# A gated MLP of a perceiver block: part of gate and up by seven products of halves, and a triangular substitution in two halves of rows

## The chip, the cores and the metric

One core of one Trainium2 chip runs the whole program in one launch. The time is the device time of one execution in microseconds (us); before the change three runs gave 2789.46 to 2791.44 us, median 2791.18. A core has a matmul engine (TensorE, in the profile PE, with its weight loads listed apart as PEld), VectorE (DVE), ScalarE (ACT), GpSimd (POOL), and SyncE (SP), which here only issues DMAs. Each engine takes its instructions in order. On-chip memory is SBUF (128 partitions) and PSUM, eight banks of 512 fp32 values per partition, where matmuls write.

## What is computed

The reference is a block of three layers over x of 128 x 32 x 512 fp32 values (4096 tokens of 512 channels), each added to x:

```python
x = x + _L0_xattn_ref(_layernorm(x), mask, ctx_2048, ctx_2048, ...)   # cross-attention
x = x + _L0_attn_ref(_layernorm(x), ...)[0]                           # delta rule, then gated MLP
x = x + _L0_ffn_ref(_layernorm(x), ...)                               # quantised FFN after a Hadamard rotation
...
h2 = _rms(x, mlp_norm_w)          # the gated MLP inside the second layer
gate = h2 @ Wgate.T               # 512 -> 1408
up = h2 @ Wup.T
x = x + silu(gate) * up @ Wdown.T
```

The delta rule is a scan over 32 time steps per sequence and head. The kernel replaces the scan by a triangular system per sequence and head (32 rows, 16 values each), solved by forward substitution.

## The kernel before

All of it is fp32 apart from the quantised FFN. The program has four stages in time: cross-attention (0 to about 617 us), the products of the delta rule (`delta_products`, to about 1090), the delta rule's outputs with the gated MLP (`delta_out_mlp`, to about 2230), and the FFN (`HadamardFfn.run`, to the end). A scheduler places the instructions that the code traces into each engine's queue, mostly in traced order, but earlier where an engine would idle. `InOrder` ties the calls that go through it to the traced order; `follow` ties two instructions; `tc.issue_after` puts what is traced in its block behind a given instruction on that instruction's engine. `mixed` interleaves generators: each yields the cost of the step that it just traced, and the one that is furthest behind its own total goes next.

The MLP stage goes over 16 blocks of 256 tokens (`TB`), two tiles of 128 each. `mlp(b)` holds the work of a block: for each of 11 chunks of 128 hidden channels (`FC`) four matmuls of gate into one PSUM tile (L1307), four of up into another (L1310), SiLU on ACT (L1312) and the product into `mT` on VectorE (L1313); then for each of the two tiles 11 matmuls of down (L1318), the addition of the input (L1323), statistics, the subtraction of the mean (L1328), two butterfly steps of the Hadamard transform (`butterflies`, L128 and L129), and two stores on GpSimd's queue (L1325, L1330). A step's cost is 3.5 for a chunk and 9.5 for a down tile.

`back(b + 1)` prepares the next block meanwhile: it loads the solved rows `u`, copies them on GpSimd into one of two block-diagonal operands `um` (L1225), multiplies with `pe` (L1243), normalises, multiplies with `wo` (L1272), adds a layer norm of x1 whose scaling is L1267, and transposes the result into `hT` (L99, L1296), of which there are two buffers. In blocks 1 to 8 `late_products` adds the last products of the delta rule (L782 to L794).

Also mixed in, behind the last VectorE instruction of the MLP (`mark`), are the substitution steps of `Substitution.solve`: for each row s a scaling of 64 values (L745), a multiply into `pr` (L749) and a subtraction from all later rows of `W` (L755), (31 - s) x 64 values each. There are eight such solves; the first and part of the second run in the product stage (where a helper records everything as L153), the others beside the MLP at a pace of 46 cost units per block (60 in the first). `L` has one buffer of 32 rows, loaded in four pieces, `W` two. In the last three blocks the FFN weights are made ternary instead: gate and up stay in SBUF (`resident`), down goes to DRAM (`fq`) and is loaded at the start of the FFN stage (L1671).

The weights of the MLP are loaded by SyncE: `wg` (two DMAs at 1060.75 us), then `wu` (at 1102.83) and `wd`; wg is scaled by the norm weights on ACT, wu on VectorE (L1368).

`Halves` already serves cross-attention: a product of matrices as seven products of halves (Strassen's method in Winograd's form), with four sums of the weight quarters computed once (`weights`, L260 to L263) and sums of the input quarters per use (`sums`). `operands` names the pair for each product; `BANK` names the PSUM bank that it is accumulated in; after products 1, 5 and 6 ACT copies the bank.

## Time and profile before

| | us |
|---|---|
| median of three runs | 2791.18 |
| profiled execution, its own time | 2793.26 |
| its span, first to last instruction | 2791.2 |
| TensorE busy | 2741.2 (98%) |
| VectorE busy | 2110.2 (76%) |
| ACT busy | 1109.5 (40%) |
| GpSimd busy | 740.2 (27%) |
| MLP stage, one block | 71.1, without late products 69.75 |
| FFN stage, one tile of 128 tokens | 17.0 |

The profile lists, per group of instructions, the line of code, engine, operation, output and inputs with their shapes, the count, busy time and the mean duration of one, and the idle time of the engine just before them with what ended it. Matmuls overlap each other, so the mean duration of one is longer than the distance from one start to the next; the order of time shows the latter. A busy TensorE says that it had work, not that it ran at its peak. The granted clock was 0.994 in the mean. Each fp32 matmul of the code shows as two records.

### The profile page before, as it was taken

The page shows a single profiled execution, that of the slowest core. Times are in us where ns is not written, and L with a number is a line of the kernel's source. Part 1 is how long each engine was busy: PE and PEld are TensorE (multiplying, and loading weights), DVE is VectorE, ACT ScalarE, POOL GpSimd, SP SyncE. Part 2 cuts the span into 40 slices and gives each one's busy share as a digit, 9 for nine tenths or more (in the row PEclk, how much of TensorE's full clock was granted, in tenths as well). Part 3 has the DMA queues.
Part 4 walks back from the last instruction along what each step waited for, and adds up shares of the span by engine and source line. Part 5 has one row for each costly group of instructions (what it writes and reads, how often), then busy time and mean ns, then how long its engine had stood idle before and what let it go on. Part 6 is the DMA issues. An engine that isn't in the chain of part 4 may idle for free.

```text
span 2791.2 us, 49070 instructions
## 1 busy us (share of the span) xinstructions
PE 2741.2 (98%) x18590; PEld 1847.2 (66%) x18590; DVE 2110.2 (76%) x3745; ACT 1109.5 (40%) x1972; POOL 740.2 (27%) x1076
## 2 busy tenths in 40 slices
PE   7999999999999999999999999999999989999999
PEld 6777788764444444766677777777777756666665
DVE  5565655546799797887878787878445599999998
ACT  2222222227777675222222222212222156666665
POOL 3222222215888785121111222111100100000000
PEclk9999999999999999999999999999999999999999
DMA  9898987774655668414141414131223434334443
GB/s 321 300 312 292 309 300 274 272 236 107 185 160 158 179 174 267 141 57 130 61 133 59 137 59 148 45 110 46 83 87 91 139 84 84 85 84 86 90 87 71
DMA packets 347482, 421.65 MB, mean 151 GB/s; under 512 B 151408, under 2 KB 256240, under 8 KB 345072
## 3 DMA queue, kind: packets, MB, share of 16 engines
q1 hardware_dynamic: 308064, 320.69, 38.2%
q0 software_dynamic: 39184, 97.83, 11.4%
q8 instruction: 148, 2.42, 0.4%
q14 instruction: 86, 0.70, 0.1%
HBM read 284.69 MB, written 90.18 MB: 134 GB/s over the span
## 4 chain that ended last, share of the span: by engine, by line
PE 90%; DVE 6%; DMA 2%; issue 1%; ACT 0%; SPq 0%; DVEq 0%; ACTq 0%
PE ps L153 39%; PE pm L1307 11%; PE pm L1310 11%; PE pm L1318 10%; PE pp L153 10%; PE ps L1272 4%; PE ps L1243 2%; PE pg L153 2%; DVE acc L153 1%; DVE W L153 1%; DMA raw<-in_f_w_gateT_dram 1%; PE pn L153 1%; PE ps L99 1%; DVE pr L153 1%; DVE m L153 0%
## 5 line engine op out<-in xcount | busy, mean ns | idle before, releaser
L1307 PE MATMUL pm<-hT,wg 128*128 128x256 f32 x1408 | 343.3, 386 | 0.2 <-ACT hT L1296 0.2
L1310 PE MATMUL pm<-hT,wu 128*128 128x256 f32 x1408 | 334.1, 380 | 4.4 <-DVE wu L1368 3.2
L1318 PE MATMUL pm<-wd,mT 128*128 128x512 f32 x704 | 307.4, 592 | 0.0
L1307 PEld LDWEIGHTS pm<-hT,wg 128*128 128x128 f32 x1408 | 263.9, 191 | 52.5 <-issue 13.0
L1310 PEld LDWEIGHTS pm<-hT,wu 128*128 128x128 f32 x1408 | 267.1, 190 | 42.7 <-DVE wu L1368 4.2
L755 DVE TENSOR_TENSOR W<-W,pr 128x1280 f32<-128x1280 f32 (+30 forms) x206 | 250.2, 1214 | 2.6
L749 DVE TENSOR_TENSOR pr<-L,W 128x1216 f32<-128x1216 f32 (+30 forms) x205 | 244.7, 1194 | 9.1 <-DMA L<-ld 5.0
L1318 PEld LDWEIGHTS pm<-wd,mT 128*128 128x128 f32 x704 | 132.4, 190 | 153.8 <-issue 152.8
L153 PE MATMUL ps<-wq,qT 128*128 128x512 bf16 x960 | 218.7, 381 | 3.9 <-ACT t L153 3.9
L1312 ACT ACTIVATE sg<-pm 128x256 f32<-128x256 f32 x176 | 66.9, 382 | 295.7 <-PE pm L1307 271.7
L153 PEld LDWEIGHTS <-qT 128*128 128x128 bf16 x960 | 94.3, 98 | 105.9 <-issue 7.0
L1663 POOL DMA_DIRECT2D xo<-x x29 | 24.6, 849 | 506.0 <-ACT xo L153 471.5
L1313 DVE TENSOR_TENSOR mT<-pm,sg 128x256 f32<-128x256 f32 x176 | 73.8, 419 | 107.4 <-PE pm L1310 90.0
L153 DVE TENSOR_TENSOR mb<-m 128x1024 f32<-128x1024 f32 x128 | 153.3, 1218 | 0.1
L479 POOL DMA_DIRECT2D vx<-vn x256 | 126.5, 500 | 96.2 <-DVE vn L418 52.0
L153 DVE TENSOR_TENSOR m<-mb 128x1024 f32<-128x1024 f32 x128 | 150.8, 1219 | 1.2
L153 ACT ACTIVATE t<-ps,magic,qs 128x512 f32<-128x512 f32 x158 | 115.7, 781 | 46.7 <-DVE qs L153 42.3
L1286 POOL TENSOR_TENSOR xs<-xs,y 128x512 f32<-128x512 f32 x32 | 41.9, 1310 | 321.7 <-DVE y L1283 309.5
L153 PEld LDWEIGHTS ps<-hd,mT 128*128 128x128 f32 x1024 | 119.1, 192 | 6.3 <-ACT mT L153 2.1
L793 POOL TENSOR_TENSOR kk<-kk,cm 128x256 f32<-128x256 f32 x128 | 121.1, 946 | 2.8
L153 PE MATMUL ps<-hd,mT 128*128 128x128 f32 x1024 | 119.6, 275 | 1.9 <-ACT mT L153 1.9
L789 POOL DMA_DIRECT2D ld<-kk x128 | 93.6, 731 | 89.9 <-ACT kk L153 61.6
(288 smaller groups left out, 5353.3 us busy)
## 6 DMA issues: line engine op xcount, KB each, us to landing
kall<-in_ctxT_dram SPq DMA_DIRECT2D x32, 2056.0 KB
cx<-in_ctx_dram SPq DMA_DIRECT2D x32, 2048.0 KB
x<-xo POOLq DMA_DIRECT2D x64, 256.0 KB, 4.9
ld<-kk POOLq DMA_DIRECT2D x128, 128.0 KB, 2.7
pd<-kk POOLq DMA_DIRECT2D x128, 128.0 KB, 2.6
L<-ld SPq DMA_DIRECT2D x32, 512.0 KB
pe<-pd SPq DMA_DIRECT2D x256, 64.0 KB
kqm<-kq SPq DMA_DIRECT2D x448, 32.0 KB
```

What stands on the lines that cost most here:

```text
L153: got = method(*args, **kw)
L479: nc.gpsimd.dma_start(vx[r : r + T, j, :], vn[j * T : (j + 1) * T, i, halves[h]])
L749: self.dve.tensor_mul(pr[:, 0:n], bc(L[:, s, :, s + 1 : T].rearrange("p h t -> p t h"), HD), w[:, s].unsqueeze(1).to_broadcast([P, n, H4, ...
L755: self.dve.tensor_sub(w[:, s + 1 :], w[:, s + 1 :], pr[:, 0:n])
L789: nc.gpsimd.dma_start(ld[r].rearrange("(i p) f -> p i f", p=P), kk[:, 0].rearrange("p i h t -> p i (h t)"))
L793: nc.gpsimd.tensor_mul(q, q, cm.unsqueeze(1).to_broadcast([P, 2 * H4, T]))
L1272: pw_last = nc.tensor.matmul(pw, oT[:, i, dc, :], wo[:, dc, :], start=dc == 0, stop=dc == DC - 1)
L1307: nc.tensor.matmul(pg, wg[:, dc, fs], hT[:, dc, :], start=dc == 0, stop=dc == DC - 1)
L1310: nc.tensor.matmul(pu, wu[:, dc, fs], hT[:, dc, :], start=dc == 0, stop=dc == DC - 1)
L1312: nc.scalar.activation(sg, pg, AF.Silu)
L1313: mark[:] = [nc.vector.tensor_mul(mT[:, fc, :], pu, sg).ins]
L1318: nc.tensor.matmul(pd, mT[:, fc, i * P : (i + 1) * P], wd[:, fc, :], start=fc == 0, stop=fc == FC - 1,)
```

## The change

In `delta_out_mlp`, the first four chunks of gate and up (512 hidden channels) are computed by the seven products; the other seven chunks stay plain, with gate and up now in one PSUM bank. The order is written out, all the MLP's matmuls and ACT calls are tied to it by `InOrder`, and the down tile yields once in its middle. The block's input sums `hs` are made at the end of `back`; `hT` has one buffer. The layer norm's scaling L1267 moves to ACT, the subtraction of the mean L1328 is folded into the first butterfly step. The weights come in the pieces that the order needs; in block 0 the four plain chunks that were loaded first go first. `Substitution.solve` works on `W` in two tiles of 16 rows (three buffers) and `L` in pieces of 8 rows (two buffers), and stores each half. `um` has one buffer. The FFN's up weights go to DRAM as the down weights did and are loaded at the start of the FFN stage. `Halves.load` and `Halves.quarters` take over what cross-attention had as local functions, with the same instructions there.

```diff
-def butterflies(nc, a, b):
+def butterflies(nc, a, b, c, twice):
...
-        nc.vector.tensor_add(o[:, :, 0, :], i[:, :, 0, :], i[:, :, 1, :])
+        if step == 1:
+            nc.vector.scalar_tensor_tensor(
+                o[:, :, 0, :], i[:, :, 0, :], twice, i[:, :, 1, :], ALU.add, ALU.add
+            )
+        else:
+            nc.vector.tensor_add(o[:, :, 0, :], i[:, :, 0, :], i[:, :, 1, :])
...
         def load(s):
-            self.sync.dma_start(L[:, s : s + some].rearrange("p s h t -> p s (h t)"), rows[:, s : s + some])
+            t = self.pool.tile([P, some, H4, T], FP, name="L", bufs=2)
+            self.sync.dma_start(t.rearrange("p s h t -> p s (h t)"), rows[:, s : s + some])
+            pieces.append(t)
...
+        for p in range(2):
+            t = self.pool.tile([P, half, H4, HD + 1], FP, name="W", bufs=3)
+            self.sync.dma_start(
+                t.rearrange("p t h v -> p t (h v)"), given[:, p * half : (p + 1) * half]
+            )
+            W.append(t)
...
+            own, k = s // half, s % half
+            row = w[own][:, k]
+            self.dve.tensor_mul(row, row, bc(W[own][:, k, :, HD], HD))
+            for p in range(own, 2):
+                a, b = max(s + 1, p * half), (p + 1) * half
+                n = b - a
+                if n == 0:
+                    continue
+                pr = self.pool.tile([P, half, H4, HD], FP, name="pr")
                 self.dve.tensor_mul(
                     pr[:, 0:n],
...
-                yield 0.3 + 0.07 * n
-                self.dve.tensor_sub(w[:, s + 1 :], w[:, s + 1 :], pr[:, 0:n])
-            yield 0.1 + 0.07 * n
+                yield 0.1 + 0.07 * n
+                rest = w[p][:, a - p * half :]
+                self.dve.tensor_sub(rest, rest, pr[:, 0:n])
+                yield 0.1 + 0.07 * n
+            if k == half - 1:
+                nc.gpsimd.dma_start(
+                    solved[:, own * half : (own + 1) * half],
+                    W[own].rearrange("p t h v -> p t (h v)"),
+                )
+                yield 0.1
...
-        wg = wp1.tile([P, DC, FF], FP, name="wg")
-        wu = wp2.tile([P, DC, FF], FP, name="wu")
+        cuts = (4 * P, 8 * P, FF)
+        rest = [
+            [
+                (wp2 if k else wp1).tile([P, DC, b - a], FP, name=f"w{n}{k}")
+                for n in range(2)
+            ]
+            for k, (a, b) in enumerate(zip(cuts, cuts[1:]))
+        ]
+        paired = [wp2.tile([P, 7, 2, 2 * P], FP, name=f"wp{n}") for n in range(2)]
...
-                nc.vector.tensor_scalar(
-                    y, xs[i], mv[:, i, 0:1], rs[:, i, 0:1], ALU.subtract, ALU.mult
+                nc.scalar.activation(
+                    y, xs[i], AF.Identity, bias=less[:, n : n + 1], scale=stats[1][:, n, 0:1]
                 )
...
+            t = wk2.tile([P, 4, 2, P], FP, name="hs", bufs=1)
+            b11, b12, b21, b22 = Halves.quarters(hT)
+            nc.vector.tensor_sub(t[:, 1], b12, b11)
+            nc.vector.tensor_sub(t[:, 2], b22, b12)
+            nc.vector.tensor_sub(t[:, 0], b22, t[:, 1])
+            nc.vector.tensor_sub(t[:, 3], b21, t[:, 0])
...
+            def gated(out, pg, pu, sg):
+                act_mlp.activation(sg, pg, AF.Silu)
+                mark[:] = [nc.vector.tensor_mul(out, pu, sg).ins]
+
+            def plain(fc):
+                k, at = divmod(fc - 4, 4)
+                bank = psm.tile([P, 2, TB], FP, name="pm")
+                for n in range(2):
+                    for dc in range(DC):
+                        pe_mlp.matmul(
+                            bank[:, n], rest[k][n][:, dc, at * P : (at + 1) * P], hT[:, dc, :],
+                            start=dc == 0, stop=dc == DC - 1,
+                        )
+                gated(mT[:, fc, :], bank[:, 0], bank[:, 1], wk2.tile([P, TB], FP, name="sg"))
+                return 3.5
+
+            def product(k):
+                name = Halves.BANK[k]
...
+                for n in range(2):
+                    a, c = ops[n][k]
+                    for m in range(2):
+                        for j in range(2):
+                            pe_mlp.matmul(
+                                bank[:, n, m], a[:, j, m * P : (m + 1) * P], c[:, j],
+                                start=first and n + m + j == 0, stop=n + m + j == 3,
+                                skip_group_check=not first,
+                            )
+                if k in (1, 5, 6):
+                    kept[k] = wk2.tile([P, 2, 2, P], FP, name="kept", bufs=3)
+                    act_mlp.copy(kept[k], bank)
+                return 1.75
+
+            def summed(name, k):
+                nc.vector.tensor_add(kept[k], banks[name], kept[k])
+                return 0.0
+
+            def quarter(i, j, src, sg):
+                gated(mT[:, 2 * i : 2 * i + 2, j * P : (j + 1) * P], src[:, 0], src[:, 1], sg)
+                return 0.0
...
+            if b == 0:
+                for _ in range(4):
+                    yield plain(chunks.pop(0))
+                prepared()
+                order = order[4:] + order[:4]
+            yield product(2)
+            yield product(5)
+            yield product(1) + summed("a", 1)
+            yield plain(chunks.pop(0))
+            yield product(6) + quarter(0, 0, kept[1], kept[1][:, 0])
+            yield product(3) + summed("c", 6)
+            yield plain(chunks.pop(0))
+            yield product(7) + summed("b", 5) + quarter(0, 1, kept[6], kept[6][:, 0])
+            yield plain(chunks.pop(0)) + quarter(1, 1, kept[5], kept[5][:, 0])
+            if chunks:
+                yield plain(chunks.pop(0))
+            yield product(4) + last_quarter()
+            for fc in chunks:
+                yield plain(fc)
             for i in range(NTL):
                 pd = psm.tile([P, D], FP, name="pm")
...
+                    if n == FC // 2:
+                        yield 5.0
...
-                nc.vector.tensor_scalar(z, xo, mv2[:, n, 0:1], None, ALU.subtract)
-                z = butterflies(nc, z, zp.tile([P, D], FP, name="zb"))
+                nc.vector.tensor_scalar_mul(twice, mv2[:, n, 0:1], -2.0)
+                z, zb = (zp.tile([P, D], FP, name=n) for n in ("z", "zb"))
+                z = butterflies(nc, xo, zb, z, twice)
                 nc.gpsimd.dma_start(z2[n * P : (n + 1) * P, :], z)
-                yield 9.5
+                yield 4.5
...
+        def prepared():
+            for w, mul, engine in zip(paired, muls, (nc.gpsimd, nc.vector)):
                 for dc in range(DC):
+                    rows = w[:, dc // 2 : 4 : 2, dc % 2]
+                    mul(rows, rows, nw[:, dc : dc + 1])
+                Halves.weights(nc, w, engine)
...
             wd = wp2.tile([P, IC, D], BF, name="wq2")
+            wu = wp2.tile([P, DC, IF], BF, name="wq1")
+            nc.sync.dma_start(wu.rearrange("p c n -> p (c n)"), wu_dram)
...
-        um = [up.tile([P, H // 2, 2, 2 * HD], FP, name=f"um{i}") for i in range(2)]
+        um = [up.tile([P, H // 2, 2, 2 * HD], FP, name=f"um{i}") for i in range(1)]
```

The block's total in `mixed` falls from 3.5 x 11 + 9.5 x 2 = 57.5 to 3.5 x 7 + 1.75 x 7 + 9.5 x 2 = 55.75. The pools of the MLP stage are reordered so that `mT` lies last.

## The prediction

> **What bounds the kernel now.** I read first the chain of waits (by engine and line), then busy time by stage, then TensorE's (PE's) order of time in the MLP stage, and last who waited for whom there.
>
> ```profile
> PE 90%; DVE 6%; DMA 2%; issue 1%; ACT 0%; SPq 0%; DVEq 0%; ACTq 0%
> L1307 PE MATMUL pm<-hT,wg 128*128 128x256 f32 x1408 | 343.3, 386 | 0.2 <-ACT hT L1296 0.2
> L1310 PE MATMUL pm<-hT,wu 128*128 128x256 f32 x1408 | 334.1, 380 | 4.4 <-DVE wu L1368 3.2 <-DVE mT L1313 1.2
> ```
>
> TensorE sets the end in nine tenths of the span, and in the whole MLP stage it waits 4.6 us before gate and up matmuls. So a removed matmul is worth its full spacing, as long as VectorE (DVE) keeps up. Whether it can is read by block (columns: PE, weight load, DVE, ACT, POOL busy):
>
> ```profile
> 1212.45:1283.56 71.11, 71.11 (x409) 49.78 (x409) 63.07 (x100) 15.76 (x29) 11.40 (x12) 1.00 0.18 58
> 1283.56:1354.66 71.10, 71.10 (x409) 49.77 (x409) 55.03 (x81) 15.86 (x29) 14.02 (x21) 1.00 0.43 135
> 1780.09:1849.84 69.75, 69.75 (x378) 49.43 (x377) 57.76 (x105) 14.74 (x27) 5.27 (x7) 1.00 0.25 82
> ```
>
> A block lasts 71.1 us (69.75 without the late products) and PE is busy in all of it; VectorE has 8 to 16 us left. The price of the matmuls that go and of those that come stands in PE's order of time, the first two lines from a block, the other three from cross-attention's query and key products, which already have the new shape:
>
> ```profile
> 1504.05 1.89 PE L1307 MATMUL pm<-hT,wg 128*128 128x256 f32 x8
> 1505.78 1.89 PE L1310 MATMUL pm<-hT,wu 128*128 128x256 f32 x8
> ...
> 424.08 1.06 PE L153 MATMUL ps<-hT,wq 128*128 128x128 f32 x8
> 424.97 1.06 PE L153 MATMUL ps<-hT,wk 128*128 128x128 f32 x8
> 425.87 1.06 PE L153 MATMUL ps<-hs,wq 128*128 128x128 f32 x8
> ```
>
> What counts is start to start: eight 256-column matmuls every 1.73 us (216 ns each), eight 128-column ones every 0.895 us (112 ns). Each fp32 matmul of the code shows as two.
>
> **The change, part by part.**
>
> *Matmuls.* Per block, four chunks of gate and up go: 4 x 2 x 4 x 2 = 64 records, 64 x 215.7 ns = 13.80 us. Seven products come: 7 x 16 = 112 records of 128 columns, 112 x 111.7 ns = 12.51 us. The difference is 1.29 us, in 16 blocks 20.6 us. Bounds: half of the 256-column spacing is 107.8 ns (12.07 us, 27.7 us in all); the group of hT,wq has 69.8 us for 512, 136 ns each (15.3 us, a loss of 23 us in all), but that counts the drained tail wherever another shape follows. The unbroken run of 14 such groups decides: 111.7.
>
> Here a rule speaks against the change. The Trainium skill, page "TensorE: Matmul & The Clock Gate", section "Back-to-back issue gap", says that the sustained spacing of matmuls does not fall in proportion to the columns, since every one brings a weight load: about 81 ns at 128 columns and 131 ns at 512. By that ratio, 98 ns at 256 by a straight line (an estimate from that page), half the columns would cost 83% and the products would lose some 6 us per block. The trace shows 52% for fp32; the measurement stands.
>
> *Evacuation and sums.* Per block three ACT copies of 128x512 come (the kept row of cross-attention, 0.586 us) and two normalisations move from L1267 to ACT (0.806, the row of xt): 3.4 us more on an engine busy for 16 of 71. On VectorE L1267 goes (2 x 0.46 start to start) and so does L1328 (2 x 0.40); there come three sums of 128x512 from PSUM (0.61 each), four differences of 128x256 (0.33 to 0.42), two small scalings (0.1) and a slightly dearer first butterfly (0.05, twice): 1.8 + 1.5 + 0.2 + 0.1 - 1.7 = +1.9 us per block. On the path they cost nothing while they end under other matmuls: product 6 waits for ACT's copy of bank b, with a plain chunk (3.45 us) between; product 4 waits for VectorE's sum from b, with two (6.9 us). Without that cover each would cost what VectorE is behind, up to one substitution step of 2.2 us.
>
> *Four differences at a block's end.* Product 5, second in the fixed order, needs the first of them, 1.8 us after the block begins. The last transposes now come between the halves of the second down tile, 4 us before its end, and VectorE idles in that place today (6.6 us before xo). I take 0; bounds 0 and what stands if they queue behind the xo tail and one substitution step: 0.61 + 0.60 + 0.2 + 1.4 + 2.2 - 1.8 = 3.2 us per block.
>
> *Substitution.* Steps 0 to 14 issue one more pair of multiply and subtract. Elements stay. A pair costs 0.17 us (intercept of 128x64 against 128x1024 rows, 0.155 us each, less 0.07 overlap) to 0.39 (both wait, as from L749 to L755): 2.6 to 5.9 us on some 86 per solve. The planner's sum falls from 82 to 78.8, so every unit of pace carries 7 to 11% more work: +3.0 to +4.8 us in a block, where it was 44.8. With +1.9, VectorE goes from 58.0 (mean of blocks 1 to 10) to 62.9 to 64.7 of 69.8, and 68 to 70 in the fullest. It fits because the down tile's matmuls are now left at half, which puts substitution steps where VectorE idles:
>
> ```profile
> 1447.60 2.09 DVE L749 TENSOR_TENSOR pr<-L,W 128x1856 f32<-128x1856 f32 x1
> 1449.61 0.16 DVE L1292 RECIPROCAL r<-r 128x2 f32<-128x2 f32 x1
> 1456.38 0.69 DVE L1323 TENSOR_TENSOR xo<-pm,xs 128x512 f32<-128x512 f32 x1 [6.62 <-PE pm L1318]
> ```
>
> For fullest blocks I put +3 us in all (0 to 20: 1.7 in each of twelve). In the product stage, where the chain runs on VectorE between 853 and 941 us, 1.6 solves have 4 to 9 us more work, of which a part shows: +2 (0 to 8).
>
> *First block.* PE waits 3.24 us at 1112.82 for the scaling of wu, whose load is issued at 1102.83 behind the product stage's buffers; the two groups after it run at 0.66 to 0.83 of the clock, 2.2 us over 1.73 each. The first four chunks of both weights now lie together where wg lay (issued at 1060.75), so this goes: -5. In its place the paired weights must be loaded, scaled and summed before product 5: 3.5 MB from 1103 at about 330 GB/s to 1113.6, four ACT scalings of 0.7, two of GpSimd's 1.3 us (L260 to L263): about 1119; PE arrives after four chunks and the block's state matmuls at 1120 to 1122. +1 (0 to 5). Sum -4 (-7 to +5).
>
> *One um buffer instead of two.* GpSimd may copy for the block's second tile only after the first tile's matmuls; 12 us lie between the two (1543 to 1555) and the copy takes 0.5 to 2.3. Queued behind it on GpSimd are ld and pd stores and the xs sums; ahead of it may stand a ud store that waits for VectorE (10.5 us at 1563.93), now two per solve. +2 (0 to 10).
>
> *Handover to the last stage.* The up weights (2 MB) come back from DRAM. Their SBUF is free when the last block's last chunk is done, 19 us before PE gets there; 1.5 MB of wu landed in 9 us. Hidden: +1. If SyncE issues it only after the transpose of q0 at 2228.0, it lands at about 2237 against a first use at 2231.5: +6. Waiting behind it on SyncE are the zt loads, four of which were issued at 2166.
>
> *One bank for gate and up.* The Trainium skill, page "PSUM — Partial Sum Buffer", section "PSUM bank collisions raise a hardware error", asks that two engines be kept off one bank, so the SiLU should now wait for up too, 1.73 us later. By the trace that delays ACT, which idles 272 us for L1307, and each chunk now takes one bank of five instead of two. By the rule one chunk per block could show this, by the trace none; the sum has 0.
>
> **Sum.** -20.6 - 4 + 2 + 3 + 2 + 1 = -16.6. From the profiled execution's span of 2791.2 (its own time is 2793.26; the runs' median, 2791.18, lies at the span) that gives 2775 us; its own bounds are 2762 (the start's full gain and matmuls a little under 111.7) and 2785.
>
> **Rivals.**
> 1. *VectorE becomes the bound in the substitution blocks.* For: 64.7 us plus 3.3 us of waits for ACT's square roots plus the 6.6 us in the down tile, if it stays idle, is 74.6, over 71.1. Against: the half-way yield; blocks 12 to 15 have only 25 to 47 us on VectorE. Place: blocks 1 to 11. It decides where a block's VectorE work and waits pass 71.1 by more than the 1.3 saved elsewhere; at 74.6 it gives 11 x 3.5 = +38, with the five other blocks (-6) and the small terms about 2820, at half of it some 2800. Chance 0.17.
> 2. *The wait moves to the block's start:* product 5 stands for the differences, 1.3 to 3.2 us in 15 blocks. 2.0 gives 30 - 20.6 = +9, about 2800; below 1.3 it does not make a loss. Against: VectorE's idle time just before. Chance 0.09.
> 3. *The gain is eaten in small waits* (um, bank, first block, handover, product stage at their upper bounds: 10 + 5 + 6 + 8, without the start's gain), -20.6 + 3 + about 16: 2789. Chance 0.12.
> 4. *128-column matmuls do not keep 112 ns between other shapes:* at 123 the saving is gone, 2796 without the start's gain. Against: 14 groups in a row. It is part of 3.
>
> **How the numbers follow.** The forecast has 0.62. Two runs of this kernel can be told apart from about 0.2%, 5.6 us: faster is below 2785.6. Faster takes the forecast and a little of 3, 0.65; the same, most of 3 and the edges, 0.11; slower, rivals 1 and 2 with a rest, 0.24. The range, 2762 to 2804, holds the forecast, rival 3, rival 2 and the lower half of rival 1.
>
> **What would show it.** Right: blocks of about 69.8 us (68.5 without late products), 112 records per block of 128 columns spaced 112 ns, no wait of PE on DVE in them, DVE at 63 to 65 us per block, wu gone from PE's waits at the start. Wrong: PE waits named after VectorE's sums, the differences or mT (rivals 1 and 2), after GpSimd's um or paired weights, or after the wu load at the handover; and blocks that get no shorter though nothing waits (rival 4).

## The result and the profile after

The changed kernel takes 2819.32 us (median of 4, 2815.24 to 2826.01) where the kernel before takes 2791.31 (median of 4): a ratio of 1.0103, 95% interval 1.0079 to 1.0126. It is slower by 28 us; 2775 was predicted. The profiled execution took 2816.41 with a span of 2814.6, 23.4 us over the span before. A cut by landmarks on TensorE says where the 23.4 are:

| us | before | after | difference | predicted |
|---|---|---|---|---|
| start to first chunk of gate in the MLP stage | 1104.8 | 1115.2 | +10.4 | +2 |
| first chunk to end of the last down matmul | 1124.9 | 1129.2 | +4.3 | -19.6 (matmuls, first block, substitution, um) |
| from there to the end | 561.4 | 570.2 | +8.8 | +1 |

Of the first row's 10.4 us, 2.1 stand ahead of the product stage, in code that did not change: the stage's first store of a kk tile begins at 646.0 before and at 648.1 after.

The chain of waits, by engine, had 90% TensorE and 6% VectorE before. After:

```profile
PE 64%; DVE 23%; DMA 6%; issue 3%; ACT 2%; POOL 1%; SPq 0%; ACTq 0%; DVEq 0%; POOLq 0%
```

VectorE now sets the end in a quarter of the span. Busy time by stretch, from the first wo matmul of one block to that of the next (columns: PE, weight load, DVE, ACT, POOL busy; granted clock; DMA share; GB/s):

```profile
1220.60:1295.45 74.85, 69.92 (x457) 50.50 (x456) 70.99 (x130) 19.38 (x37) 11.41 (x15) 1.00 0.34 98
1366.89:1442.44 75.55, 71.39 (x457) 51.70 (x456) 65.41 (x130) 18.71 (x35) 11.04 (x16) 0.98 0.32 99
1442.44:1513.11 70.67, 69.54 (x457) 50.34 (x456) 58.59 (x91) 18.37 (x33) 14.68 (x18) 1.00 0.33 88
1589.42:1658.69 69.27, 69.27 (x458) 50.44 (x457) 61.56 (x102) 18.91 (x34) 12.48 (x16) 1.00 0.27 81
2007.56:2075.47 67.91, 67.91 (x425) 49.94 (x424) 25.49 (x62) 18.29 (x32) 6.93 (x10) 1.00 0.25 71
```

The reader is to see two things. Where nothing disturbs it, a block takes 67.91 us (69.27 with late products), 1.84 less than before: the matmuls gained even more than predicted. And four stretches with late products take 74.9 to 76.7, though TensorE is busy for only 69.9 to 71.6 us in them and VectorE for 64.5 to 65.4 in three (in the first, 71.0 of 74.9, it is nearly full). Who TensorE waited for, from 1100 to 2260 us (us in total, times, longest):

```profile
PE pm L158 <- ACT kept L158: 13.8, 6, 5.1
PE ps L158 <- DMA wq<-fq: 8.4, 1, 8.4
PE pm L158 <- ACT kk L816: 6.0, 4, 2.7
PE pm L158 <- DVE wp L1483: 4.8, 1, 4.8
...
PE pm L158 <- DVE wp L277: 1.4, 1, 1.4
```

L158 is the line of the helper that records the tied calls (L153 before). The kept copies are ACT's copies of the products' banks, kk (L816) is ACT's copy of a late product, wq<-fq the load of the FFN's up weights, wp the pairing of the weights in the first block. The end of one block and the start of the next, in order of time:

```profile
1404.89 10.72 SPq L1246 DMA_DIRECT2D xs<-x  x2
1405.27 4.46 PE L158 MATMUL pm<-wd,mT 128*128 128x512 f32 x10
...
1414.57 0.69 DVE L1433 TENSOR_TENSOR xo<-pm,xs 128x512 f32<-128x512 f32 x1
...
1418.22 0.81 ACT L1308 ACTIVATE y<-xs,less,rs 128x512 f32<-128x512 f32 x1 [8.72 <-DMA xs<-x]
1418.94 0.56 ACT L816 COPY kk<-pm 128x512 f32<-128x512 f32 x1
1419.55 3.72 PE L158 MATMUL pm<-hT,w 128*128 128x256 f32 x16 [1.36 <-ACT kk L816]
1421.91 0.57 ACT L158 COPY kept<-pm 128x512 f32<-128x512 f32 x1
...
1424.95 0.59 ACT L816 COPY kk<-pm 128x512 f32<-128x512 f32 x1 [2.47 <-DMA pd<-kk]
1425.43 0.59 ACT L158 COPY kept<-pm 128x512 f32<-128x512 f32 x1
...
1426.07 1.23 PE L158 MATMUL pm<-hs,wp 128*128 128x128 f32 x6 [2.80 <-ACT kept L158]
```

The last down matmul ends at 1409.73. VectorE adds its tile (xo) only at 1414.57, 4.8 us later. VectorE alone, in between:

```profile
1409.23 1.02 DVE L774 TENSOR_TENSOR pr<-L,W 128x832 f32<-128x832 f32 x1
1410.28 1.03 DVE L781 TENSOR_TENSOR W<-W,pr 128x832 f32<-128x832 f32 x1
1411.23 0.42 DVE L1341 TENSOR_TENSOR hs<-hT 128x256 f32<-128x256 f32 x1
1411.56 0.22 DVE L767 TENSOR_TENSOR W<-W 128x64 f32<-128x64 f32 x1
1411.70 0.42 DVE L1342 TENSOR_TENSOR hs<-hT 128x256 f32<-128x256 f32 x1
1412.03 0.95 DVE L774 TENSOR_TENSOR pr<-L,W 128x768 f32<-128x768 f32 x1
1412.90 0.42 DVE L1343 TENSOR_TENSOR hs<-hT,hs 128x256 f32<-128x256 f32 x1
1413.23 0.95 DVE L781 TENSOR_TENSOR W<-W,pr 128x768 f32<-128x768 f32 x1
1414.11 0.42 DVE L1344 TENSOR_TENSOR hs<-hT,hs 128x256 f32<-128x256 f32 x1
1414.44 0.22 DVE L767 TENSOR_TENSOR W<-W 128x64 f32<-128x64 f32 x1
1414.57 0.69 DVE L1433 TENSOR_TENSOR xo<-pm,xs 128x512 f32<-128x512 f32 x1
```

xo stands behind substitution steps (pr, W) and behind the change's own four differences (hs), which are 1.7 us of these lines; they overlap a little. At the ends of the four long stretches' blocks the differences take 1.3 to 1.7 us of the 3.2 to 4.8 that xo is late. xo frees the buffer that the second xs load waits for; y, which the change moved to ACT, waits for that load till 1418.22; and in ACT's queue behind y stand the late product's copy, which TensorE needs for a bank, then a copy of a product, then the second kk copy, which waits until the first has been stored out of the one kk buffer, and only then product 1's copy, for which product 6 stands 2.80 us.

### The profile page after: what moved, and what is told of

Read it like the earlier page. It is cut to its first block, busy times and chain, and to the rows that moved or that the text cites. A ratio compares the mean times of both kernels' runs of the same rounds, so it can differ in the third digit from the quotient of the medians.

```text
span 2814.6 us, 50889 instructions
## 1 busy us (share of the span) xinstructions
PE 2724.5 (97%) x19295; PEld 1862.8 (66%) x19358; DVE 2173.9 (77%) x4072; ACT 1158.9 (41%) x2056; POOL 744.1 (26%) x1104
## 4 chain that ended last, share of the span: by engine, by line
PE 64%; DVE 23%; DMA 6%; issue 3%; ACT 2%; POOL 1%; SPq 0%; ACTq 0%; DVEq 0%; POOLq 0%
PE ps L158 37%; PE pm L158 19%; DVE pr L774 4%; DVE W L781 4%; PE pp L158 4%; DVE acc L158 3%; DVE W L158 2%; PE ps L1313 2%; DVE pr L158 2%; PE ps L1283 1%; DMA vd<-vt 1%; DVE mT L1357 1%; DMA pd<-kk 1%; DVE m L158 1%; DVE W L767 1%
## 5 line engine op out<-in xcount | busy, mean ns | idle before, releaser
L158 PE MATMUL pm<-hT,w 128*128 128x256 f32 x1792 | 407.8, 382 | 6.4 <-ACT kk L816 6.0
L158 PEld LDWEIGHTS pm<-hT,w 128*128 128x128 f32 x1792 | 335.4, 191 | 58.2 <-issue 7.4
L158 PE MATMUL pm<-wd,mT 128*128 128x512 f32 x704 | 310.0, 592 | 0.0
L774 DVE TENSOR_TENSOR pr<-L,W 128x1024 f32<-128x1024 f32 (+15 forms) x298 | 266.4, 894 | 5.2
L781 DVE TENSOR_TENSOR W<-W,pr 128x1024 f32<-128x1024 f32 (+15 forms) x299 | 260.7, 872 | 3.8
L158 PEld LDWEIGHTS pm<-wd,mT 128*128 128x128 f32 x704 | 131.2, 190 | 146.2 <-issue 140.6
L158 PE MATMUL ps<-wq,qT 128*128 128x512 bf16 x930 | 215.5, 379 | 6.2 <-ACT t L158 4.6
L158 PEld LDWEIGHTS <-qT 128*128 128x128 bf16 x960 | 94.0, 98 | 105.3 <-issue 5.5
L158 DVE TENSOR_TENSOR mb<-m 128x1024 f32<-128x1024 f32 x128 | 153.3, 1218 | 0.1
L1357 DVE TENSOR_TENSOR mT<-pm,sg 128x256 f32<-128x256 f32 x128 | 53.8, 421 | 128.0 <-ACT sg L158 127.8
L158 DVE TENSOR_TENSOR m<-mb 128x1024 f32<-128x1024 f32 x128 | 150.8, 1220 | 1.2
L158 PE MATMUL pm<-hs,wp 128*128 128x128 f32 x1024 | 130.9, 282 | 15.2 <-ACT kept L158 13.8
L158 PEld LDWEIGHTS pm<-hs,wp 128*128 128x128 f32 x1024 | 126.3, 197 | 24.5 <-ACT kept L158 16.2
L158 ACT ACTIVATE t<-ps,magic,qs 128x512 f32<-128x512 f32 x158 | 115.6, 781 | 48.4 <-DVE qs L158 44.1
L158 PEld LDWEIGHTS ps<-hd,mT 128*128 128x128 f32 x1024 | 119.1, 192 | 6.9 <-ACT mT L158 2.8
L158 PE MATMUL ps<-hd,mT 128*128 128x128 f32 x1024 | 119.7, 275 | 2.3 <-ACT mT L158 2.3
L158 ACT ACTIVATE sg<-pm 128x256 f32<-128x256 f32 x128 | 48.4, 383 | 177.8 <-PE pm L158 176.1
L158 PE MATMUL ps<-wq,q2T 128*128 128x512 bf16 x481 | 114.1, 379 | 2.6 <-DMA q2T<-q 0.9
L1313 PE MATMUL ps<-wo,oT 128*128 128x512 f32 x256 | 116.2, 594 | 0.0
```

The lines of the kernel that those rows point to most:

```text
L158: got = method(*args, **kw)
L774: self.dve.tensor_mul(pr[:, 0:n], bc(L[:, s % some, :, a:b].rearrange("p h t -> p t h"), HD), row.unsqueeze(1).to_broadcast([P, n, H4, HD]),)
L781: self.dve.tensor_sub(rest, rest, pr[:, 0:n])
L1313: pw_last = nc.tensor.matmul(pw, oT[:, i, dc, :], wo[:, dc, :], start=dc == 0, stop=dc == DC - 1)
L1357: mark[:] = [nc.vector.tensor_mul(out, pu, sg).ins]
```

## The experiments

Two theories came out of this. **A**: ScalarE's in-order queue, with y and the second kk copy ahead of the copies that the products need. Its rival **B**: VectorE has too much to do in these blocks. All edits are to the changed kernel unless another is named; each ratio is against the kernel before, run in the same set. The sets ran on three chips, on which the kernel before has medians of 2790.1 to 2793.8 us, so times of different sets are compared only to some 3 us; the ratios are free of that.

**e1, y back on VectorE.**

```diff
-                nc.scalar.activation(
-                    y, xs[i], AF.Identity, bias=less[:, n : n + 1], scale=stats[1][:, n, 0:1]
-                )
+                nc.vector.tensor_scalar(
+                    y, xs[i], stats[0][:, n, 0:1], stats[1][:, n, 0:1], ALU.subtract, ALU.mult
+                )
```

> The changed kernel with the scaling y = (x - mean) * rstd back on VectorE, as it stood before the change; nothing else differs. Theory A (ScalarE's in-order queue: y waits there for its x tile, 90.7 us in 13 waits, and the copies that product 6 needs stand behind it): about half of the 30 us lost in the seven blocks with late products comes back, 2800 to 2811 against 2819; the longest TensorE waits on ScalarE's kept and kk copies go below 3 us. Theory B (VectorE carries too much in these blocks: 32 more instructions of 0.4 us there): 2819 to 2832. Theory C (the loss hangs on the single kk buffer alone): within 3 of 2819.

2808.18 us, ratio 1.0067 (1.0043 to 1.0090). The time is in theory A's range, though a wait of 3.1 us on a kept copy was left (its profiled execution, 2816.87, is the slowest of its four).

**e2, two kk buffers.**

```diff
-        kk = pool.tile([P, 2, 2, H4, T], FP, name="kk")
+        kk = pool.tile([P, 2, 2, H4, T], FP, name=names[r])
...
-                    pd[gi, NTL * b : NTL * (b + 1), ec], k, km, cm,
+                    pd[gi, NTL * b : NTL * (b + 1), ec], k, km, cm, ("kk", "kk1"),
```

> The changed kernel with two buffers in place of one for the late products' copy kk (two small statistics tiles go from four buffers to one to make room). Theory A, its second half (the second kk copy waits up to 6.1 us on ScalarE for the store of the first, 25.1 us in 7 waits, and the kept copy of product 1 stands behind it): 10 to 20 us less than 2819, and no ScalarE wait on the pd store. Theory B (VectorE's load) and theory C' (y's wait alone): within 3 of 2819.

2803.14, ratio 1.0047 (1.0033 to 1.0061): 16 us back. The waits on kept nearly vanish, but a new one stands first (1150 to 1760 us):

```profile
PE ps L1283 <- DMA pe<-pd: 8.3, 4, 3.9
PE pm L158 <- ACT kk L816: 4.2, 4, 2.0
PE pm L158 <- ACT kept L158: 0.6, 1, 0.6
```

The pe loads are issued by SyncE behind the second xs load, which waits for xo. In the block that then took 76.9 us, xo began 5.5 us after the last down matmul. This cause lies ahead of ACT.

**e3, both edits.**

> Both edits together, y on VectorE and two kk buffers. Theory A: the seven blocks with late products take 69.3 to 71 us each in place of 71 to 77, about 25 us less than 2819, so 2790 to 2798. If the two waits hide one another, both alone give little and only this run gives the 25. Theory B: not under 2815.

2807.76, ratio 1.0064 (1.0043 to 1.0084). Theory A alone falls: with both of its waits taken away, blocks of 74.5, 75.3 and 78.2 us remain, with waits of up to 6.5 us on the pe loads.

**e5, 42 units of substitution per block in place of 46.** So theory B was made sharper (called B2 in the expectations): what counts is VectorE at the block's boundary.

```diff
-PACE = 46.0
+PACE = 42.0
```

> The changed kernel with one number other: each block of the last stage but three gets 42 units of the substitution in place of 46, so that it ends about one block later (VectorE was only 36% busy in 2000 to 2100). Theory A (ScalarE's queue alone): within 4 of 2819. Theory B2 (what is left of the loss after two kk buffers comes from VectorE: it is over 95% busy at the block boundary, its add for xo, 5.6 us behind the last down matmul in one block, holds the xs loads, and SyncE's pe loads behind them, for which TensorE then waits up to 3.9 us): 5 to 12 us less, 2807 to 2814.

2796.90, ratio 1.0022 (1.0005 to 1.0039): 22 us from one number, far more than expected. The same boundary as above, in this run:

```profile
1399.78 4.46 PE L158 MATMUL pm<-wd,mT 128*128 128x512 f32 x10
1405.49 0.69 DVE L1433 TENSOR_TENSOR xo<-pm,xs 128x512 f32<-128x512 f32 x1
1409.31 0.82 ACT L1308 ACTIVATE y<-xs,less,rs 128x512 f32<-128x512 f32 x1 [8.74 <-DMA xs<-x]
...
1412.77 1.05 ACT L158 COPY kept<-pm 128x512 f32<-128x512 f32 x2
...
1415.99 1.95 PE L158 MATMUL pm<-hs,wp 128*128 128x128 f32 x16
...
1419.74 0.59 ACT L816 COPY kk<-pm 128x512 f32<-128x512 f32 x1 [5.92 <-DMA pd<-kk]
```

xo comes 1.25 us after the down tile, y 5.1 us after it in place of 8.5. And the scheduler, with other VectorE work to place, put both kept copies ahead of the second kk copy, which now waits 5.92 us and harms nobody. Stretch by stretch (each from a block's first wo matmul to the next; the first row is how long xo starts after the last down matmul ends; order: K a kk copy, p a copy of a product, as they stand in ACT's queue behind it):

| stretch (0 is the first) | 2 | 3 | 4 | 5 | 6 | 7 | 8 |
|---|---|---|---|---|---|---|---|
| after: xo late by, us | 4.3 | 0.8 | 4.8 | 0.7 | 4.7 | 1.4 | 3.2 |
| order | KpKp | KpKp | KpKp | KppK | KpKp | KppK | KpKp |
| length, us | 74.9 | 71.4 | 75.6 | 70.7 | 76.3 | 69.3 | 76.7 |
| 42 units: xo late by, us | 3.3 | 0.7 | 1.3 | 0.9 | 1.5 | 1.2 | 0.3 |
| order | KppK | KppK | KppK | KpKp | KppK | KppK | KpKp |
| length, us | 70.3 | 69.3 | 69.3 | 70.5 | 69.8 | 69.3 | 72.3 |

The order KpKp with xo less than 1.5 us late goes with 1 to 3 us over 69.3, with a later xo 5.6 to 7.4. A late xo without that order goes with little: stretch 2 at 42 units has it, 3.3 us, and lasts 70.3, and in stretches 10 and 11 of the changed kernel, which have no late products, xo is 2.4 and 2.8 us late and they last 67.9 and 68.5. The order was read, not changed by itself. Over blocks 1 to 9, both tiles, xo is 0.50 us late before the change, 2.46 after it, 0.82 with 42 units.

**e6, 42 units and two kk buffers.**

> 42 units and two kk buffers together. Two kk buffers alone gave 2803. Theory A: within 4 of 2803. Theory A and B2 together (ScalarE's queue and VectorE's at the block boundary, each with its own share): 2790 to 2798, and the seven blocks with late products at a mean of 70 to 71 us, where two kk buffers alone had 72.

2787.57, ratio 0.9987 (0.9973 to 1.0002). The seven stretches have a mean of 69.9 (71.9 with two buffers alone), and the MLP stage takes 1102.4 us, 22.6 less than before the change: in sum as much as was predicted for it, and a little more. From 2819 both steps together give 32 us, two buffers alone 16.

**e14, 50 units**, the opposite edit.

> The changed kernel with 50 units of the substitution to a block in place of 46. 42 gave 2797 and 46 gives 2819. Theory B2 (VectorE's fullness in a block sets the loss): longer again, 2825 to 2845, the blocks with late products at 76 us or more. Rival (42 units help only by where the steps happen to fall between the block's boundaries, or by the later end): 2810 to 2822.

2824.97, ratio 1.0110 (1.0096 to 1.0123). xo is 2.76 us late in the mean; four stretches take 74 to 76 us, one of them without late products (76.2, with xo 6.9 us late). 42, 46 and 50 units give 2797, 2819 and 2825. But 50 units cannot be told from 46: the ratios are 1.0110 and 1.0103, and their intervals overlap almost whole. Nor do the blocks with late products reach the 76 us that was expected. What is shown is the step from 46 down to 42; past 46 the loss hardly grows.

**e13, more cover.**

```diff
             yield plain(chunks.pop(0))
+            if b:
+                yield plain(chunks.pop(0))
             yield product(6) + quarter(0, 0, kept[1], kept[1][:, 0])
```

> The changed kernel with one more plain chunk between product 1 and product 6 in all blocks but the first (taken from those behind product 4), all numbers as in the change. Theory A (product 6 is caught because one plain chunk of 3.45 us is too short a cover for ScalarE's copy of product 1, late by up to 6 us): 6 to 14 us less than 2819, and the waits on kept and kk under half of 19.8 us. Theory B2 (VectorE's fullness holds back the whole boundary, so that the next wait takes its place): 2813 to 2822, with TensorE's waits at other places, such as on the pe loads.

2810.76, ratio 1.0060 (1.0047 to 1.0074). 8.6 us less, in theory A's range, but the waits moved, which is nearer to B2: none on kept is left, and the plain chunks wait for banks that the late copies hold, 14.9 us where it was 6.0, so that both together do not fall under half of 19.8 (same columns, 1150 to 1760 us):

```profile
PE pm L158 <- ACT kk L816: 14.9, 7, 4.7
```

**e15, y on VectorE with 42 units and two buffers.**

> 42 units and two kk buffers, and y on VectorE again. With y on ScalarE: 2787.6. Theory (the move of y is right as long as nothing stands behind it that is late; it takes 0.8 us a block from VectorE and its waits for xs harm nothing once kk does not wait): 2788 to 2794. Rival (y's waits on ScalarE, up to 11 us, cost time in any case): 2780 to 2785.

2792.61, ratio 0.9999 (0.9990 to 1.0009): 5 us above e6 in the medians, 3 by the ratios, whose intervals overlap. So the rival is out: y's waits on ACT cost nothing that can be seen once nothing urgent is late behind them. That the move of y gains something is likely (e3 too is 5 us above e2), not shown.

**e8, the substitution in halves as the only change to the kernel before.** The new `solve` in the old kernel.

> The kernel before with the substitution in halves as the only part of the change. Theory: the price of the halves is in the product stage, where VectorE is 97% busy: that stage 3 to 5 us longer and the blocks of the last stage as before (71.1 us), so 2793 to 2797. Rival (the halves are what disturbs the blocks with late products, through VectorE's order and the three W halves): 2805 or more, with blocks of 74 us among those. Rival (the halves cost nothing): 2789 to 2793.

2806.04, ratio 1.0043 (1.0028 to 1.0059): 15 us over the kernel before, which is the first rival's range, though without its sign of blocks of 74 us: there is one. The profiled execution (span 2800.8) shows 9.6 of the 15: the first chunk starts at 1112.5 in place of 1104.8, and the MLP stage is 2.3 us longer. So most of what the profile shows is in the product stage, at twice the size expected; some 5 us of the median are not placed.

The old blocks bore the halves nearly unharmed, and this bears on theory B. Over stretches 1 to 10 the substitution keeps VectorE busy for 48.9 us a block here and for 47.9 in the changed kernel. But xo is only 0.32 us late in the mean of blocks 1 to 9 (2.46 in the changed kernel). Between 1150 and 1760 us VectorE here still stands idle 40.2 us, in 8 waits, for the down tile's matmuls ahead of xo, as before the change (47.8 us in 10); in the changed kernel it never does, with 42 units 16.6 us in 6. So more substitution work alone does not make xo late; it does so in the changed block, where it stands in the place that was idle. Which part of the changed block brings that about, the down tile's yield in the middle, the four differences or the shorter block, no run takes apart.

The price in the product stage is VectorE's. Its time on instructions that touch W, from 600 us to the first chunk (columns: length, DVE busy and count, POOL busy and count, clock, DMA share, GB/s), before and after the whole change:

```profile
600.00:1104.80 504.80, 141.38 (x129) 0.55 (x1) 0.99 0.60 168
```

```profile
600.00:1115.20 515.20, 164.44 (x183) 1.10 (x2) 0.99 0.59 164
```

23 us more in the same number of cost units. Over the whole run the substitution keeps VectorE busy for 733.4 us in 992 instructions, where it was 690.5 in 752. The planner's sum per solve, by its own formulas, fell the other way, from 82 to 78.8.

**e9, the product stage given less of it**, with two kk buffers.

```diff
-SHARE = 0.245 * SOLVE
-PACE = 46.0
+SHARE = 0.21 * SOLVE
+PACE = 43.5
```

> Two kk buffers, the product stage given 0.21 in place of 0.245 of a substitution per group, the blocks 43.5 units in place of 46 (so that it still ends in time). Counted in the two traces, the substitution in the product stage costs VectorE 165.2 us after the change and 141.4 before, with the same units; 0.21 gives some 142 again. Theory (the product stage, 97% busy on VectorE, is longer by the halves' extra instructions): the first chunk of the last stage starts 5 to 9 us earlier than the 1112 to 1116 of the runs with 0.245, the blocks as with 42 units or 1 us longer in sum of all, and the time 2779 to 2786 against 2787.6 with 42 units and two buffers. Rival (the product stage is longer for another cause, such as more waits between the halves' instructions): 1111 or more, and 2787 or more.

2781.89, ratio 0.9967 (0.9955 to 0.9978). The stage's share of the substitution is down to 147.9 us and the first chunk starts at 1099.8, 12 us earlier than in e6. So the product stage's length follows VectorE's load. The other traces agree: from the stage's first kk store to the first chunk it is 458.8 and 458.5 us in the two with the old solve, 464.9 to 470.6 in the thirteen with halves and 0.245, 452.9 and 453.7 in the two with 0.21 (e9 and e12). A side effect: stretch 1 rose to 74.1 (TensorE waited 4.65 us for um, GpSimd's copy into the one buffer).

**e11, the kernel before with 44 units.**

> The kernel before with 44 units of the substitution to a block in place of 46, nothing else (it needs at least 43.9 to end in time). Theory: its blocks were not disturbed (71.1 us each but for the first two and two of 71.4), so nothing to gain: 2789 to 2793. Rival (any such kernel gains from fewer units, and the change was only the occasion): 2785 or less.

2791.14, ratio 1.0000 (0.9990 to 1.0011). The kernel before has nothing to gain from fewer units in a block; 46 suited it and no longer suits the changed one. Whether it would gain from a share below 0.245 was not tried.

**e4, the FFN's up weights issued by GpSimd.**

```diff
-            nc.sync.dma_start(wu.rearrange("p c n -> p (c n)"), wu_dram)
+            nc.gpsimd.dma_start(wu.rearrange("p c n -> p (c n)"), wu_dram)
```

> The changed kernel with the load of the second feed-forward weight issued by GpSimd in place of SyncE, where it stood behind the transpose of q0. Theory H (the 8.40 us wait of TensorE at the start of the last part is the load's issue place): that wait goes, 7 to 9 us less than 2819. Rival (the load waits for memory that the last down matmuls still read, or for its data): within 2 of 2819, the load issued no earlier than about 2244.

2817.06, ratio 1.0092 (1.0073 to 1.0112). GpSimd issued it behind its ternary stores, 3 us before the last down matmul's end, and the wait fell to 4.7 us; from that end to the run's end took 566.5 us in place of 570.2. In the median, 2 us under the changed kernel, it cannot be told from none; the profile shows it.

**e7, both ends mended, with two kk buffers.** The load in four quarters from ACT's queue, and the second paired weight scaled by ACT.

```diff
-            for w, mul, engine in zip(paired, muls, (nc.gpsimd, nc.vector)):
+            for w, mul, engine in zip(paired, (nc.scalar.mul, nc.scalar.mul), (nc.gpsimd, nc.vector)):
...
-            nc.sync.dma_start(wu.rearrange("p c n -> p (c n)"), wu_dram)
+            for k in range(NG):
+                nc.scalar.dma_start(
+                    wu[:, :, k * D : (k + 1) * D],
+                    wu_dram.rearrange("p (c n) -> p c n", c=DC)[:, :, k * D : (k + 1) * D],
+                )
```

> Two kk buffers, and both ends of the last stage mended: the second paired weight scaled by ScalarE in place of VectorE (TensorE waited 4.8 and 1.4 us for it in the first block), and the load of the second feed-forward weight cut in four and issued by ScalarE (TensorE waited 8.4 us for it whole; issued whole by GpSimd 3 us ahead of the last down matmul's end it was still 4.7). Theory: 4 to 6 us at the first end and 6 to 8 at the second, so 2789 to 2794 against 2803 with two buffers alone. Rival (the time is only moved, as the next thing is late too: the pe loads in the first block, the z tiles behind the weight): 2798 or more.

2799.73, ratio 1.0029 (1.0016 to 1.0043). The far end gave its 5 us (565.0 after the last down matmul). In the first block the wait only moved, as the rival said: 6.0 us for the weights' sums on VectorE (L277), which stood between substitution steps.

**e10, the pairing put ahead of the first block in the program**, on the engines of the change, with the four quarters, 42 units and two buffers.

```diff
-                prepared()
...
+        prepared()
         for b in range(NBL):
```

> 42 units, two kk buffers, the second feed-forward weight's load in four parts from ScalarE's queue, and the paired weights' scaling and sums put ahead of the first block's work in the program, on the engines of the change. With 42 units and two buffers: 2787.6. The mended ends of the last run gave 5.1 us at the feed-forward (570.1 to 565.0 after the last down matmul) and nothing in the first block, where TensorE waited 6.0 us for the sums in place of 4.8 and 1.4. Theory (in the first block VectorE interleaves the pairing with the substitution, which is only a matter of order): 4 to 6 us there too, so 2777 to 2780. Rival (the weights land too late in any order): 2781 to 2784, and a wait of 4 us or more in the first block.

2777.59, ratio 0.9953 (0.9939 to 0.9967). The order of the program was the cure: the first block's wait for the pairing is 1.3 us, with the weights' loads issued only some 2 us earlier. At the handover the four quarters cost TensorE 4.0 us in all, in 4 waits. The handover after (the kernel of the change) and here:

```profile
2243.07 1.20 SPq L1620 DMA_TRANSPOSE q0T<-q  x1
...
2244.62 0.34 SPq L1697 DMA_DIRECT2D wq<-fq  x1
...
2254.15 1.44 PE L158 MATMUL ps<-wq,q0T 128*128 128x512 bf16 x3 [8.40 <-DMA wq<-fq]
```

```profile
2208.28 2.73 ACTq L1698 DMA_DIRECT2D wq<-fq  x4
...
2212.67 1.02 PE L158 MATMUL ps<-wq,q0T 128*128 128x512 bf16 x4 [0.60 <-DMA wq<-fq]
```

**e12, everything that helped:** two kk buffers, 0.21 and 43.5 units, pairing ahead, four quarters.

> Everything that helped, together: two kk buffers, 0.21 of a substitution per group in the product stage and 43.5 units to a block, the paired weights prepared ahead of the first block, the feed-forward weight in four loads from ScalarE's queue. If the gains add up: 2777.6 (with 42 units and 0.245) less the 5.7 that 0.21 with 43.5 gave over 42 units (2787.6 to 2781.9), so 2770 to 2774. Rival (the product stage's gain and the first block's are the same time, as the first block got slower with 0.21, its second 74.1 us in place of 66.9): 2775 to 2779.

2773.34 (median of 5), ratio 0.9930 (0.9918 to 0.9943): 46 us under the changed kernel and 20 under the kernel before, so faster than both, and the gains added up. What is left of TensorE's waits between 1130 and 1760 us is, but for 1.1 us, one that did not show until e9, for the single um buffer:

```profile
PE ps L1283 <- POOL um L1265: 7.7, 4, 5.0
```

## Why the prediction was wrong

**Matmuls, -20.6: right, too small.** Counted start to start in an undisturbed block, gate and up went from 38.57 us to 24.27 for the plain chunks and 12.88 for the products, 1.42 less (predicted 1.29). The products' matmuls stand 115 to 116 ns apart, not 111.7, and the 256-column ones that went cost more than 215.7: 38.57 / 176 = 219. Another 0.33 comes from the um products, which now run 64 in a row, and 0.10 from the transposes. Rival 4 is out.

**Evacuation and sums, "on the path they cost nothing while they end under other matmuls": the first step that failed.** The cover was named (product 6 behind one plain chunk of 3.45 us) and the price without it too, but not what could make ACT late. ACT was costed as busy time, "3.4 us more on an engine busy for 16 of 71". The text named nothing that would stand ahead of the copies in ACT's queue: y with its wait for a load (up to 10.9 us), and the kk copies with their wait for a store, which also existed before (31.5 us in 8 waits) and harmed nobody then. e2 priced the second at 16 us.

**"It fits because the down tile's matmuls are now left at half, which puts substitution steps where VectorE idles": the second.** The prediction took VectorE's 6.6 us of idleness ahead of xo for free room, and put the four differences there too, at 0. That idleness is what made xo prompt: with it gone, xo is 2.46 us late in the mean, in place of 0.50, and the chain of waits shown above begins with it. e8, with as much substitution in the old block, keeps the idleness and has xo 0.32 us late.

**Substitution: the work was nearly right for a block, the price was not.** "+3.0 to +4.8 us in a block" was forecast; over stretches 1 to 10 the substitution keeps VectorE busy for 47.9 us in the mean, 45.1 before, and everything on VectorE 62.7 (62.9 to 64.7 forecast). The price taken for it, +3 us in all, supposed that VectorE costs nothing until a block is full. With late products it costs when xo at the boundary is late, well before that. e5 and e6 show it: some 16 us with two buffers (2803 to 2788).

**Product stage, "+2 (0 to 8)": mis-sized, +7.7 by e8.** It was reckoned from the extra pairs alone, 4 to 9 us more work; 23 us came (16%). The 7 to 11% more work per unit, stated in the same paragraph for the blocks, was left out there. Two parts are seen: 183 instructions are 1.48 solves where 129 were 1.37, and a whole solve keeps VectorE busy for 91.7 us in place of 86.3.

**First block, -4: mis-sized.** The wait for wu went (3.2 us), one of 4.8 and one of 1.4 came. The engines' durations were reckoned, not the steps that the substitution puts between VectorE's; and the paired weights, reckoned from 1103, were issued from 1114.65 on.

**Handover, +1: the second branch came true**, "+6 if SyncE issues it only after the transpose of q0"; +8.8 came. The load was issued 1.55 us after that transpose began and took 9.5 from issue to use; TensorE waited 8.4 us.

**um and the one bank: no wait of TensorE in the changed kernel is named after them**, but um costs up to 5.0 us at once when the rest is out of the way (e12). **The four differences, 0:** product 5 never waits for them, but they stand ahead of xo; their share of the loss was not measured by itself.

**Rivals.** Rival 1 (VectorE, "about 2820") is closest, and was given 0.17: right in the engine and, by luck, in the size. It put 3.5 us on each of blocks 1 to 11; four stretches have 5.6 to 7.4 over 69.3, the other three with late products 0 to 2. Its mechanism, a block filled up, does not fit three of the four: VectorE was busy for 64.5 to 65.4 of some 76 us. In the fourth, 71.0 of 74.9, it may have a part. In the others VectorE acts through one late instruction and two queues behind it. Rival 2, a wait at the block's start for the differences, did not appear there; the waits were on product 6 and the plain chunk before it. Two sums of the rivals do not come out: rival 3's four bounds add up to 29, not to about 16, which gives 2803; and rival 4's 2796 has most of the start's gain in it, without which it is some 2800.

## What to carry to other kernels

An engine that is 85% busy need not have 15% to spare: ask when its one urgent instruction at a stage's boundary comes, and list what stands behind everything that waits for it, queue by queue. When an instruction is moved to an idle engine, its wait moves too, and so do the things behind it; the busy share of that engine says nothing about that. When the work per cost unit changes, planner constants that were tuned with the old work are a part of the change; here two such numbers, one buffer, a call's place in the program and a load cut in four on another queue turned a loss of 28 us into a gain of 20. And idle time ahead of an urgent instruction is not free room: what is put there, the instruction waits for.

## What the hardware showed that was not expected

A stall of TensorE can cost more than its length. Three stretches of the changed kernel (columns as in the table of stretches): an idle time of 2.73 us ended by a wait on kk, the chunk behind it, and the matmuls behind a wait of 5.08 us:

```profile
1564.75:1567.50 2.75, 0.07 (x1) 0.00 (x0) 2.72 (x8) 1.29 (x3) 0.54 (x1) 1.00 0.55 180
1567.55:1571.00 3.45, 3.45 (x16) 2.95 (x16) 3.31 (x9) 0.95 (x2) 2.20 (x3) 1.00 0.59 206
1718.64:1722.40 3.76, 3.76 (x20) 3.54 (x24) 3.53 (x5) 0.23 (x1) 1.97 (x3) 0.50 0.87 253
```

After 2.73 us of idleness the granted clock stays at 1.00 and the chunk takes its usual 3.45 us; after 5.08 it is 0.50 for 3.8 us, and a product that takes 1.89 us from its start to the next (1414.35 to 1416.24) takes 3.71. The wait of 2.80 us at 1426 is already followed by a clock of 0.58 in the mean for 3.3 us. So the waits on kept, 13.8 us in all, cost more than 13.8, by about half of the slow stretches behind two of them (an estimate from these rows: 3 us). The Trainium skill, page "TensorE: Matmul & The Clock Gate", section "Part 1: The HAM clock gate", has the clock fall to half after an idle window of about 3.4 us; in this case 2.80 us were enough once and 2.73 were not.
